# Two graph layers on one core: left weight sums queued behind evictions, and a last block worked by quarters

## The chip, the cores and the metric

The kernel runs on one core of one Trainium2 chip. The metric is the device time of one execution in microseconds; of several runs the median is taken. A core has TensorE (PE; PEld is its weight load), VectorE (DVE), ScalarE (ACT), GpSimd (POOL) and SyncE (SP). SP, ACT and POOL also issue DMAs.

## The reference, cut to what matters

128 graphs of 64 nodes with 768 features, all float32. Two layers, each with a residual and a layer norm. The first layer weighs neighbours by the similarity of the features; the second is an attention of 12 heads of 64 features, masked by the same adjacency.

```python
# layer 0: x is 128 x 64 x 768, adj 128 x 64 x 64 (zeros and ones)
p = softmax(x @ x.T / sqrt(768)); delta = p * adj
attn = delta / (sum(delta) + 1e-10)
ctx = upper(attn) @ (x @ Wl.T + bl) + diag(attn) * (x @ Ws.T + bs) + lower(attn) @ (x @ Wr.T + br)
x = layernorm(x + relu(layernorm(ctx, 1e-12) * gamma + beta), 1e-5)
# layer 1: q, k, v in 12 heads
s = q @ k.T / 8 + beta1 * adj, or -9e15 where adj is 0
x = layernorm(x + heads(softmax(s) @ v), 1e-5)
```

## The kernel before

The 8192 rows are cut into 16 blocks (`NBLK`) of 512 rows; a block is 4 tiles (`T`) of 128 rows, and a tile holds two graphs of 64 rows.

**Products by seven.** A block times a 768x768 weight is cut into 2x2 parts and formed by seven products instead of eight (`seven`, L365), in the order `ORDER` = 1, 2, 6, 5, 7, 4, 3, each for two halves of 128 rows (`j` = 0, 1). That makes 14 steps; a step is named below by product and half, as (7,1), and the steps are also counted as places 0 to 13. Products 1, 6, 7 and 4 gather in one PSUM bank per half (X), products 2, 5 and 3 in another (Y). After products 1, 6 and 7 VectorE reads X into an SBUF tile `u` (`first`, L413 to L416); the product that follows in that bank has to wait for this. After products 2, 7, 4 and 3 `last` writes a finished part. For this the kernel needs sums of the parts of each weight: `prepare` (L198) loads four quarters of a weight, and `formed` (L231) makes sums 5, 6, 7 and 4 on VectorE, in three instructions where a matrix lies in three pieces (L234) and in one where it is whole (L236). `store` sends them to DRAM for later blocks.

**Order of work.** Every step ends in `step()` (L137), which takes work from three queues: `first`, `urgent` and `lazy`. A plain item is VectorE work, and only one such item is taken per step; items marked `act`, `gap` or `tiny` can go beside it; an item marked `root` waits until `urgent` has no `act` item left; an item marked `free` is taken for nothing. `settle(key)` empties the queues up to a key, and `freed()` empties `first`. Hooks of a step are called ahead of its matmuls. The first blocks are traced for the Tile scheduler, which moves instructions of an engine by when it takes them to be ready; `tc.issue_after(ins)` fixes that what is traced in it goes behind `ins` on that engine, in issue order only. The last sums of the self weights are bound so already (`formed7`, L242). From L1022 on the order is the written one.

**The start.** The attention of block 0, the self part of block 0 (`self_part(0)`), during whose steps the sums of the self weights, the softmax of block 0 and then the sums of the left weights leave the queues (`prepare("l", wst, prep, (2, 1, 0))`, with two idle items ahead of sum 5 and one ahead of sum 6), then the left part (`side_part(0, "l")`) and the right part.

**The last block** (n = 15). `projected` forms q and k for three groups of heads (`hg`); `scores` (L817) multiplies them, VectorE scales, masks and shifts, ScalarE takes the exponentials in 16 pieces of 32x256 (L853), written transposed by 32x32 blocks, and VectorE transposes within the blocks (L857). `values` (L761) forms v by the seven products. The weighted sums multiply 64x64 weights of a graph with 64 rows of v and a column of ones; two graphs of a tile lie in the two halves of the partitions. Before the change v has to have head parity, not the graph, in its partition half. In earlier blocks three copies of ScalarE swap this; in the last block `values(..., in_place=True)` evicts in quarters of 64x192 instead (L779):

```python
for r in range(2):
    for g in range(2):
        rows = slice(g * L, (g + 1) * L)
        nc.vector.tensor_tensor(v[r * L : (r + 1) * L, t, g, heads, 0:HD],
                                pairs(ps)[rows, r], add[rows, r], ALU.add)
```

`weighted` (L866) does one group of heads for tiles 0 and 1 or for tiles 2 and 3; `added` then takes a reciprocal of the ones' sums (L888) and four instructions 128x64 that divide and add to the residual (L892), for each of two PSUM tiles. Two of six such calls are hooks of the values (places 12 and 13), four come after. `finish_by_act` normalises tiles on ScalarE (sums L937, squares L940, root L918, norm L926) with stores by POOL (L930): block 14 as `lazy` work in the last values, then tiles 2 and 3 of block 15. `finish` does tiles 0 and 1 on VectorE (statistics L353, aggregate L354, norm L950) with stores by SP (L951).

The functions that the change touches, and their callers:

Of the kernel before, what the change touches and what calls it, by code (L numbers as in the profile page):

```python
# [17 lines left out]
P = 128  # L18
# [5 lines left out]
T = 4  # L24
# [27 lines left out]
def gnn_two_layers(ctx: ExitStack, tc, x, adj, wl, bl, ws, bs, wr, br, gamma, beta,  # L52
# [145 lines left out]
    def prepare(nm, quarter_pool, sum_pool, waits=(0, 0, 0), queue=lazy):  # L198
# [30 lines left out]
                                        in_=in_sbuf[i][1][:, :, hg * P : (hg + 1) * P])  # L229

        def formed(i, out, left, right):  # L231
            if any(a[1] is None for a in (out, left, right)):
                for k in range(HC):
                    nc.vector.tensor_tensor(out[0][k], left[0][k], right[0][k], ALU.subtract)  # L234
            else:
                nc.vector.tensor_tensor(out[1], left[1], right[1], ALU.subtract)  # L236
            store(i)

        def idle():
            pass  # L240
# [517 lines left out]

        return one, two

    def values(n, hooks={}, in_place=False):  # L761

        def pairs(a):
            return a.rearrange("p (j r d) -> p r j d", r=2, d=HD)

        def last(t, h, ps, part):  # L770
            add = pairs(bias["v"][:, h * HALF : (h + 1) * HALF] if part is None else part)
            heads = slice(h * 3, (h + 1) * 3)
            if not in_place:
                nc.vector.tensor_tensor(v[:, t, :, heads, 0:HD], pairs(ps), add, ALU.add)
                return
            for r in range(2):
                for g in range(2):
                    rows = slice(g * L, (g + 1) * L)
                    nc.vector.tensor_tensor(v[r * L : (r + 1) * L, t, g, heads, 0:HD],  # L779
                                            pairs(ps)[rows, r], add[rows, r], ALU.add)  # L780

        by_tokens("v", blocks[n]["S"], last, None, hooks)
        if not in_place:
            low, high = v[0:L, :, 1, :, 0:HD], v[L:P, :, 0, :, 0:HD]
            swap = l0t.tile([P, T, HP, HD], F32, tag="lr", name="swap")
            later(("v", n), act(lambda: nc.scalar.copy(swap[0:L], high)), act(lambda: nc.scalar.copy(high, low)),
                  act(lambda: nc.scalar.copy(low, swap[0:L])), queue=urgent)
# [29 lines left out]
    def scores(n, hg, at_once=1, pool=None, gaps=1):  # L817

        blk = blocks[n]
        q, k = blk["qk"]
        settle("e")
# [21 lines left out]
        def exponentials(groups):  # L845
            if 0 in groups:
                blk["eT", hg] = (pool or l1e_p).tile([P, T, 2, P], F32, tag="lr" if pool else "eT", name="eT")
            e = blk["eT", hg].rearrange("p t c i -> p (t c) i")
            for a in groups:
                rows = slice(a * Q, (a + 1) * Q)  # L850
                for b in range(P // Q):
                    cols = slice(b * Q, (b + 1) * Q)
                    nc.scalar.activation(e[cols, :, rows], pairs[rows, :, cols], AF.Exp)  # L853

        def turn(h):
            e = blk["eT", hg][:, h * 2 : h * 2 + 2].rearrange("p t c i -> p (t c i)")
# [6 lines left out]
              *[act(partial(exponentials, range(a, a + at_once))) for a in range(0, P // Q, at_once)], *[GAP] * gaps,  # L863
              *([partial(turn, 0), partial(turn, 1)] if pool is None else [lambda: (turn(0), turn(1))]), queue=urgent)

    def weighted(n, hg, halves=range(2), heads=range(2)):  # L866


        blk = blocks[n]
        settle(("v", n))  # L870
        settle(("e", n, hg))
        freed()
        xt, eT = blk["x"], blk["eT", hg]
        y = {(r, h): ps_mm.tile([P, 2, 2, HD + 1], F32, tag="mm", name=f"ps_y{r}") for h in halves for r in range(2)}
        for h in halves:
            for t in range(2):
                for c in heads:
                    for r in range(2):
                        rows = slice(r * L, (r + 1) * L)
                        for g in range(2):  # L880
                            cols = slice(g * L, (g + 1) * L)
                            nc.tensor.matmul(y[r, h][cols, t, c, :], lhsT=eT[rows, 2 * h + t, c, cols],  # L882
                                             rhs=v[rows, 2 * h + t, g, hg + c * HC, :], start=True, stop=True)

        def added(h, r):
            ps = y[r, h][:, :, heads[0] : heads[-1] + 1, :]
            rz = st.tile([P, 2, 2], F32, tag="rz1", name="rz1")[:, :, 0 : len(heads)]
            nc.vector.reciprocal(rz, ps[:, :, :, HD])  # L888
            for t in range(2):
                res = xt[2 * h + t].rearrange("p (c k r d) -> p r c k d", c=2, k=HC, r=2)  # L890
                for k, c in enumerate(heads):
                    nc.vector.scalar_tensor_tensor(res[:, r, c, hg, :], ps[:, t, k, 0:HD], rz[:, t, k : k + 1],  # L892
                                                   res[:, r, c, hg, :], ALU.mult, ALU.add)

        later(("y", n, hg), *[partial(added, h, r) for h in halves for r in range(2)], queue=first)

    def finish_by_act(n, tiles=range(T), queue=urgent):

        xt, key = blocks[n]["x"], ("f", n)
        total, nm, var, std, rstd, shift = (st.tile([P, T], F32, tag=f"f{k}", name=f"f{k}") for k in range(6))  # L900
        some = slice(tiles[0], tiles[-1] + 1)

        def sums(fs):
            if queue is lazy:
                unused = l0t.tile([P, 2, D], F32, tag="lr", name="unused")[:, 0, :]
            else:
                unused = l1s_p.tile([P, T * 4 * L], F32, tag="s", name="unused")[:, 0:D]
            for t in tiles:
                fs(t, unused)

        def mean():
            nc.vector.tensor_scalar(nm[:, some], total[:, some], -1.0 / D, None, ALU.mult)

        def variance():
            nc.vector.tensor_scalar(std[:, some], var[:, some], 1.0 / D, 1e-5, ALU.mult, ALU.add)

        def root():
            nc.scalar.activation(std[:, some], std[:, some], AF.Sqrt)  # L918

        def factors():  # L920
            nc.vector.reciprocal(rstd[:, some], std[:, some])
            nc.vector.tensor_tensor(shift[:, some], nm[:, some], rstd[:, some], ALU.mult)

        def norm(ts):
            for t in ts:
                nc.scalar.activation(xt[t], xt[t], AF.Identity, bias=shift[:, t : t + 1], scale=rstd[:, t : t + 1])  # L926

        def stored(ts):
            for t in ts:
                nc.gpsimd.dma_start(out=out_t[n, t], in_=xt[t])  # L930

        def act(f):
            return f, "act" if queue is urgent else "root"

        settle(("y", n, 0))
        settle(("y", n, 1))
        later(key, (partial(sums, lambda t, o: nc.scalar.activation(o, xt[t], AF.Identity,  # L937
                                                                    accum_out=total[:, t : t + 1])), "after"),
              GAP, GAP, tiny(mean),
              act(partial(sums, lambda t, o: nc.scalar.activation(o, xt[t], AF.Square, bias=nm[:, t : t + 1],  # L940
                                                                  accum_out=var[:, t : t + 1]))),
              GAP, GAP, tiny(variance), act(root), GAP, tiny(factors),
              *[act(partial(norm, tiles[k : k + 2])) for k in range(0, len(tiles), 2)],
              (partial(stored, tiles[0:2]), "free"), GAP, GAP, (partial(stored, tiles[2:]), "free"), queue=queue)

    def finish(n, tiles=range(T)):
        xt = blocks[n]["x"]

        def norm(t, mean, rstd):
            nc.vector.tensor_scalar(xt[t], xt[t], mean, rstd, ALU.subtract, ALU.mult)  # L950
            nc.sync.dma_start(out=out_t[n, t], in_=xt[t])  # L951

        for t, mr in zip(tiles, moments(("f", n), [xt[t] for t in tiles], 1e-5, urgent)):
            later(("f", n), partial(norm, t, *mr), queue=urgent)

# [66 lines left out]
    for n in range(NBLK):  # L1024
# [20 lines left out]
        if p >= 0:  # L1045
# [2 lines left out]
            at(one, 5, weighted, p, 1)  # L1048
            if not last and m < DEEP:
                at(left, 13, weighted, p, 2)  # L1050
                at(right, 0, finish_by_act, p)
            elif not last:
                at(right, 1, weighted, p, 2)
                at(right, 2, finish_by_act, p)
            else:
                at(qk[1], 5, weighted, p, 2)

# [92 lines left out]
        for hg in range(NHG):  # L1150
            projected(n, hg, qk[hg])

    n = NBLK - 1
    values(n, {0: [partial(finish_by_act, n - 1, queue=lazy)], 4: [partial(scores, n, 2, 2, l0t)],
               12: [partial(weighted, n, 0, (1,))], 13: [partial(weighted, n, 1, (1,))]}, True)
    settle(("f", n - 1))
    settle(("y", n, 0))
    settle(("y", n, 1))
    weighted(n, 2, (1,))
    settle(("y", n, 2))  # L1160
    finish_by_act(n, range(2, 4))
    step()
    for hg in range(NHG):
        weighted(n, hg, (0,))
        settle(("y", n, hg))
        step()
        step()
    finish(n, range(2))
    settle(("f", n))


# [29 lines left out]
```

## Time and profile before

| what | us |
|---|---|
| median of 3 runs | 2934.7 |
| lowest and highest run | 2934.53, 2936.67 |
| profiled execution | 2938.14 |
| its span, first to last instruction | 2936.4 |
| TensorE busy | 2879.9 (98%) |
| VectorE busy | 1989.5 (68%) |
| ScalarE busy | 1123.6 (38%) |
| GpSimd busy | 729.9 (25%) |
| mean granted TensorE clock | 0.995 of full speed |

Times inside the kernel are counted from the start of the span. The busy time of an engine is a sum over stages with different limits; so the stages are read one by one below. A fp32 matmul shows as two passes ("x12" is six matmuls), and the ends of matmuls are modelled, so starts are compared with starts.

### The profile page before, as it was taken

Reading aid. Unit: us, or ns where it says so; the run is one execution under the profiler, and the core shown is the slowest. Engines: PE = TensorE matmul, PEld = TensorE weight load, DVE = VectorE, ACT = ScalarE, POOL = GpSimd, SP = SyncE. Lnnn points to the kernel's source line nnn. Section 1 sums busy time; section 2 is a strip of 40 time slices with the busy share of each in tenths; the row PEclk is TensorE's granted clock in tenths of the full one; section 3 lists DMA queues with packets and bytes.
Section 4 is the critical chain, followed back from the end, with each engine's and each line's share of the span. In section 5 each row is a group of like instructions: output and inputs, shape, how many; then the busy total and the mean of one; then the engine's idle time right before and its main releaser. Section 6 shows DMA issues by size and latency. Waiting matters only on the chain.

```text
span 2936.4 us, 49944 instructions
## 1 busy us (share of the span) xinstructions
PE 2879.9 (98%) x17578; PEld 1935.1 (66%) x17578; DVE 1989.5 (68%) x4034; ACT 1123.6 (38%) x2114; POOL 729.9 (25%) x879
## 2 busy tenths in 40 slices
PE   8999999999999999999999999999999999999997
PEld 5657567585665856658576575766757567585685
DVE  5678677676676766667667576666767667676656
ACT  0004324354243543434444344443434424354254
POOL 3133122304132130411405124051230413313110
PEclk9999999999999999999999999999999999999998
DMA  9788786849578595775958759486694966849442
GB/s 322 221 274 276 234 233 194 249 138 290 154 197 248 144 285 152 214 231 163 271 147 239 203 175 271 135 260 183 185 260 137 282 163 198 244 139 287 140 127 90
DMA packets 440278, 613.18 MB, mean 209 GB/s; under 512 B 53584, under 2 KB 416720, under 8 KB 440032
## 3 DMA queue, kind: packets, MB, share of 16 engines
q1 hardware_dynamic: 362096, 493.57, 56.0%
q10 hardware_dynamic: 60848, 44.05, 8.2%
q0 software_dynamic: 17088, 72.37, 6.7%
q8 instruction: 143, 2.34, 0.3%
q14 instruction: 103, 0.84, 0.1%
HBM read 539.43 MB, written 77.27 MB: 210 GB/s over the span
## 4 chain that ended last, share of the span: by engine, by line
PE 91%; ACT 3%; POOL 2%; DVE 2%; DMA 1%; issue 1%; SPq 0%; ACTq 0%; DVEq 0%
PE ps_X L384 35%; PE ps_Y L384 26%; PE ps_Y L638 11%; PE ps_X L638 10%; PE ps_ctx L677 3%; ACT eT L853 2%; PE sc L835 2%; PE ps_y L882 2%; PE u L527 2%; POOL q L337 1%; ACT L853 1%; ACT uqk L804 1%; POOL q L336 0%; PE ps_x L286 0%; DVE o L892 0%
## 5 line engine op out<-in xcount | busy, mean ns | idle before, releaser
L384 PE MATMUL ps_X<-xT,wqk 128*128 128x256 f32 x1728 | 395.9, 381 | 9.6 <-ACT uqk L804 9.6
L853 ACT ACTIVATE eT<-s 32x256 f32<-32x256 f32 x768 | 317.8, 414 | 184.7 <-DVE s L862 174.6
L384 PEld LDWEIGHTS ps_X<-xT,wqk 128*128 128x128 f32 x1728 | 325.8, 190 | 67.1 <-ACT uqk L804 16.2
L317 POOL TENSOR_TENSOR S<-hT 128x768 f32<-128x768 f32 x16 | 28.9, 1808 | 1133.4 <-PE ps_Y L384 1102.2
L384 PE MATMUL ps_Y<-S,wqk 128*128 128x256 f32 x1152 | 264.3, 379 | 0.0
L682 ACT ACTIVATE unused<-o 128x768 f32<-128x768 f32 x60 | 50.6, 843 | 500.4 <-DVE o L679 304.9
L384 PEld LDWEIGHTS ps_Y<-S,wqk 128*128 128x128 f32 x1152 | 218.9, 190 | 29.8
L438 DVE TENSOR_TENSOR lr<-ps_Y,u_deep 128x384 f32<-128x384 f32 x273 | 152.1, 557 | 108.6 <-PE ps_Y L638 82.8
L638 PE MATMUL ps_Y<-wlr,q 128*128 128x384 f32 x546 | 208.6, 491 | 0.0
L384 PE MATMUL ps_X<-wv,xT 128*128 128x384 f32 x576 | 195.0, 489 | 0.0
L804 ACT ACTIVATE uqk<-ps_X,bq 128x256 f32<-128x256 f32 x144 | 68.3, 474 | 324.9 <-PE ps_X L384 323.7
L812 DVE TENSOR_TENSOR q<-ps_Y,uqk 128x256 f32<-128x256 f32 x144 | 61.0, 424 | 177.7 <-ACT uqk L804 89.4
L384 PE MATMUL ps_X<-ws,hT 128*128 128x384 f32 x540 | 179.4, 486 | 0.1
L892 DVE SCALAR_TENSOR_TENSOR o<-ps_y,rz,o 128x64 f32<-128x64 f32 x768 | 165.0, 277 | 6.8
L638 PE MATMUL ps_X<-wlr,q 128*128 128x384 f32 x364 | 151.1, 497 | 14.5 <-POOL q L337 5.9
L384 PEld LDWEIGHTS ps_X<-wv,xT 128*128 128x128 f32 x576 | 108.2, 190 | 80.8 <-issue 8.4
L438 DVE TENSOR_TENSOR u_deep<-ps_X,lr 128x384 f32<-128x384 f32 x195 | 107.3, 550 | 68.0 <-PE ps_X L638 66.4
L384 PEld LDWEIGHTS ps_X<-ws,hT 128*128 128x128 f32 x540 | 102.4, 190 | 71.8 <-DMA ws<-in_L_gnn_W_self_dram 0.7
L638 PEld LDWEIGHTS ps_Y<-wlr,q 128*128 128x128 f32 x546 | 101.6, 190 | 67.2
L415 DVE TENSOR_TENSOR u<-ps_X,bv 128x384 f32<-128x384 f32 x96 | 53.4, 556 | 130.3 <-PE ps_X L384 130.2
L384 PE MATMUL ps_X<-S,wqk 128*128 128x256 f32 x576 | 138.2, 385 | 0.0
L384 PE MATMUL ps_Y<-xT,wqk 128*128 128x256 f32 x576 | 135.6, 385 | 0.0
(247 smaller groups left out, 5482.6 us busy)
## 6 DMA issues: line engine op xcount, KB each, us to landing
wlr<-lr_d SPq DMA_DIRECT2D x819, 192.0 KB, 3.5
wqk<-qk_d SPq DMA_DIRECT2D x672, 192.0 KB, 2.4
wv<-d_v SPq DMA_DIRECT2D x192, 192.0 KB, 3.3
ws<-d_s SPq DMA_DIRECT2D x180, 192.0 KB, 6.0
wv<-in_L_gnn_Wv_dram SPq DMA_DIRECT2D x144, 192.0 KB, 4.1
ws<-in_L_gnn_W_self_dram SPq DMA_DIRECT2D x135, 192.0 KB, 5.5
xa<-in_x_dram SPq DMA_DIRECT2D x64, 384.0 KB, 5.4
out_dram<-o POOLq DMA_DIRECT2D x62, 384.0 KB, 6.2
```

Of the source, the lines that this page charges most:

```text
L384: nc.tensor.matmul(ps, lhsT=a, rhs=b, start=(c == 0 and i in (1, 2, 5)), stop=(c == len(fs) - 1), skip_group_check=True)
L415: recent["u"] = evicted[nm] = nc.vector.tensor_tensor(u, ps, bias[nm][:, b * HALF : (b + 1) * HALF], ALU.add)
L438: nc.vector.tensor_tensor(dst, view(ps), add, ALU.add)
L527: nc.tensor.matmul(u[g * L : (g + 1) * L, t, :], lhsT=xT[:, c, tok], rhs=xT[:, c, tok], start=(c == 0), stop=(c == KC - 1))
L638: nc.tensor.matmul(ps, lhsT=a, rhs=b, start=(k == 0 and j in (1, 2, 5)), stop=(k == len(fs) - 1), skip_group_check=True)
L677: nc.tensor.matmul(ps[g * L : (g + 1) * L, 0:HALF], lhsT=blk["aT"][:, t, g * L : (g + 1) * L], rhs=blk["lr"][t][:, g, cols], start=True, s ...
L804: nc.scalar.activation(u, ps, AF.Identity, bias=bias["qk"[j]][:, c : c + 1])
L812: nc.vector.tensor_tensor(dst, ps, part, ALU.add)
L835: nc.tensor.matmul(sc[r][g * L : (g + 1) * L, t, c, :], lhsT=q[rows, c, tok], rhs=k[rows, c, tok], start=True, stop=True)
L853: nc.scalar.activation(e[cols, :, rows], pairs[rows, :, cols], AF.Exp)
L882: nc.tensor.matmul(y[r, h][cols, t, c, :], lhsT=eT[rows, 2 * h + t, c, cols], rhs=v[rows, 2 * h + t, g, hg + c * HC, :], start=True, stop= ...
L892: nc.vector.scalar_tensor_tensor(res[:, r, c, hg, :], ps[:, t, k, 0:HD], rz[:, t, k : k + 1], res[:, r, c, hg, :], ALU.mult, ALU.add)
```

## The change

Three things are changed. The sums of the left weights are bound, with `tc.issue_after`, behind the eviction that was traced last when they leave the queue. In the last block v stays with its graph in the partition half (evictions of 128x384), and the exponentials are written so that the weights match it; the weighted sums go by quarters (two tiles, half of the features), of which three are called from hooks of the values (places 10, 11, 13) and one after; each quarter divides with two 128x384 instructions of VectorE into a tile `shares`, and adds of 128x384 by POOL or VectorE bring it to the residual; the scores of the last group are called at place 2 instead of 4. The statistics of all four tiles are taken by VectorE, nearly all behind the last eviction, and normalised by ScalarE (three tiles) and VectorE (one). The stores of the last block and of block 14 are all issued by SP, and block 14's squares no longer wait for the exponentials. `finish_by_act` becomes `finish`; for the other blocks its order and its engines stay.

```diff
         def formed(i, out, left, right):
+            with tc.issue_after(recent["u"].ins) if nm == "l" else ExitStack():
+                subtracted(out, left, right)
+            store(i)
...
-    def values(n, hooks={}, in_place=False):
+    def values(n, hooks={}, stay=False):
...
-            if not in_place:
-                nc.vector.tensor_tensor(v[:, t, :, heads, 0:HD], pairs(ps), add, ALU.add)
-                return
-            for r in range(2):
...
+            nc.vector.tensor_tensor(v[:, t, :, heads, 0:HD], pairs(ps), add, ALU.add)
...
-                    nc.scalar.activation(e[cols, :, rows], pairs[rows, :, cols], AF.Exp)
+                    to = (b, a) if n < NBLK - 1 else (a // 2 * 2 + b % 2, b // 2 * 2 + a % 2)
+                    to = [slice(k * Q, (k + 1) * Q) for k in to]
+                    nc.scalar.activation(e[to[0], :, to[1]], pairs[rows, :, cols], AF.Exp)
...
-                nc.gpsimd.dma_start(out=out_t[n, t], in_=xt[t])
+                (nc.sync if ends else nc.gpsimd).dma_start(out=out_t[n, t], in_=xt[t])
...
+        if ends:
+            begin = (summed, "after"), GAP, (lambda: (mean(), squared()), "act"), GAP, GAP, tiny(variance), act(root), GAP, GAP, GAP, tiny(factors)
...
+    def quarter(h, c):
...
+        y = [ps_mm.tile([P, 2, NHG, HD + 1], F32, tag="mm", name=f"ps_y{r}") for r in range(2)]
+        for r in range(2):
+            for k in range(NHG):
+                for t in range(2):
+                    for g in range(2):
+                        rows = slice(g * L, (g + 1) * L)
+                        nc.tensor.matmul(y[r][rows, t, k, :], lhsT=blk_e[k][rows, 2 * h + t, c, r * L : (r + 1) * L],
+                                         rhs=v[rows, 2 * h + t, r, c * HC + k, :], start=True, stop=True)
...
+        def divided(r):
+            rz = small[:, 2 * h : 2 * h + 2, 32 + 8 * c + 4 * r : 32 + 8 * c + 4 * r + NHG]
+            nc.vector.reciprocal(rz, y[r][:, :, :, HD])
+            nc.vector.tensor_tensor(by_head[:, :, r], y[r][:, :, :, 0:HD],
+                                    rz[:, :, :, None].to_broadcast([P, 2, NHG, HD]), ALU.mult)
+
+        def added(t, engine):
+            res = xt[2 * h + t][:, c * HALF : (c + 1) * HALF]
+            engine.tensor_tensor(res, res, share[:, t, :], ALU.add)
...
+    def behind(h, c):
...
+        later(("q", h, c), partial(divided, 0), lambda: (divided(1), added(0, nc.gpsimd), added(1, nc.gpsimd)),
+              queue=first)
...
+    def before_last():
+        divided, added = quarter(1, 0)
+        measured(0, 0)
+        divided(0)
+        divided(1)
+        added(0, nc.gpsimd)
+        added(1, nc.vector)
...
-    values(n, {0: [partial(finish_by_act, n - 1, queue=lazy)], 4: [partial(scores, n, 2, 2, l0t)],
-               12: [partial(weighted, n, 0, (1,))], 13: [partial(weighted, n, 1, (1,))]}, True)
+    values(n, {0: [partial(finish, n - 1, queue=lazy)], 2: [partial(scores, n, 2, 2, l0t)],
+               10: [partial(behind, 0, 0)], 11: [partial(behind, 1, 1)],
+               12: [freed], 13: [before_last]}, True)
     settle(("f", n - 1))
-    settle(("y", n, 0))
-    settle(("y", n, 1))
-    weighted(n, 2, (1,))
-    settle(("y", n, 2))
-    finish_by_act(n, range(2, 4))
-    step()
-    for hg in range(NHG):
-        weighted(n, hg, (0,))
...
+    divided, added = quarter(0, 1)
+    for t, c in ((3, 1), (2, 1), (1, 0)):
+        measured(t, c)
+    for t in (3, 2):
+        measured(t, 0)
+        whole(t)
+    factors(slice(2, 4))
+    divided(0)
+    inverse(slice(2, 4))
+    for t in (3, 2):
+        norm_by_act(t)
+    divided(1)
+    added(1, nc.gpsimd)
+    added(0, nc.vector)
+    for t in (0, 1):
+        measured(t, 1)
+        whole(t)
+    factors(slice(0, 2))
+    inverse(slice(0, 2))
+    nc.vector.tensor_scalar(xt[0], xt[0], mv[:, 0, 0:1], rstd[:, 0], ALU.subtract, ALU.mult)
+    nc.sync.dma_start(out=out_t[n, 0], in_=xt[0])
+    norm_by_act(1)
```

`measured(t, c)` is one statistics instruction over half a tile, `whole` its aggregate, `factors` adds epsilon and takes the root on ScalarE, `inverse` takes the reciprocal and the shift, and `norm_by_act` normalises on ScalarE and issues the store by SP.

## The prediction

> **What bounds the kernel now.** I read the page first, then the timeline and the granted clock of the first 60 us, then the chain that ended last and the timeline from 2880 us on, since the diff touches only these two ends.
>
> ```profile
> PE 2879.9 (98%) x17578; PEld 1935.1 (66%) x17578; DVE 1989.5 (68%) x4034; ACT 1123.6 (38%) x2114; POOL 729.9 (25%) x879
> ```
>
> TensorE is busy in 98% of the span, so between the ends only its work counts. The 56 us in which it is not busy, and the stretches in which its clock is low, are what a change of order can win. The timeline of the start (start, duration, engine, line, operands; in brackets the idle time before and its releaser):
>
> ```profile
> 29.72 1.49 DVE L234 TENSOR_TENSOR t_l<-b_l 128x384 f32<-128x384 f32 x3
> 31.78 4.14 PE L384 MATMUL ps_X<-b_s,hT 128*128 128x384 f32 x12
> ...
> 34.46 1.03 DVE L234 TENSOR_TENSOR t_l<-b_l,t_l 128x384 f32<-128x384 f32 x2 [0.80 <-DMA b_l<-in_L_gnn_W_left_dram]
> 35.40 1.49 DVE L234 TENSOR_TENSOR b_l<-b_l 128x384 f32<-128x384 f32 x3
> ...
> 36.81 1.49 DVE L234 TENSOR_TENSOR t_l<-b_l,t_l 128x384 f32<-128x384 f32 x3
> 38.22 0.55 DVE L415 TENSOR_TENSOR u<-ps_X,bs 128x384 f32<-128x384 f32 x1
> ...
> 38.82 7.16 PE L384 MATMUL ps_X<-t_s,hT 128*128 128x384 f32 x12 [2.90 <-DVE u L415]
> ...
> 49.68 4.03 PE L384 MATMUL ps_X<-b_l,hT 128*128 128x384 f32 x12
> ```
>
> The matmuls of product 7 of the self part are through at 35.9, but its eviction (L415) stands behind the sums of the left weights (L234) on VectorE, some of them waiting for a load, until 38.22. TensorE waits 2.9 us and then takes 7.16 us for 12 passes that take 3.87 us from start to start elsewhere. The granted clock of four stretches (busy us per engine, then clock, DMA share) shows why:
>
> ```profile
> 36.00:39.00 3.00, 0.18 (x1) 0.18 (x2) 2.97 (x7) 0.00 (x0) 2.33 (x5) 0.85 1.00 367
> 39.00:46.00 7.00, 7.00 (x13) 3.87 (x14) 1.93 (x4) 0.00 (x0) 0.96 (x3) 0.58 1.04 402
> ```
>
> The end, by the chain that ended last (start, duration, what):
>
> ```profile
> 2898.66 1.95 PE ps_X L384 x6
> 2900.63 0.57 DVE u L415
> ...
> 2909.71 2.15 PE ps_Y L384 x6
> ...
> 2924.18 0.86 DVE o L892 x4
> ...
> 2931.05 0.68 DVE o L950
> ```
>
> From 2900.6 on the end is nearly all VectorE: quartered evictions of the values (L779, 4 x 0.36), then normalised sums of the last block (L892), then statistics. TensorE ends its values at 2914.6; the other 21.8 us of the span have no product of a weight left.
>
> **The change, part by part. Sums of the left weights.** The 12 instructions of L234 (0.5 us each) stay; each group of three now follows the eviction traced last before it. By the queue's rules (one VectorE item per step; the self sums, then the softmax, then two idle items) the groups come at the steps of (7,1), (4,1), (3,0), (3,1): product, half. So the second eviction of product 6 runs at 29.8 instead of 33.1, the first of product 7 at 33.9 instead of 38.2, and product 4, due at 16.19 + 10 x 1.935 = 35.5, finds its bank read. All 14 steps then run without a gap: 16.19 + 14 x 1.935 = 43.3 where the left part starts, against 49.7: 6.4 us, of which 3.3 are the slow passes (7.16 - 3.87) and 3.1 idle. The moved 6 us of VectorE lie beside products 4, 3 and the left part's first (VectorE worked 4.3 us of 39 to 54). Of what waits for them: the left part needs the sum of its product 6 at 43.3 + 7.7 = 51.0, and it is formed by about 42; the stores of these sums by POOL move back by some 8 us, with the copy `lr_d<-d_l` and the stores `d_r<-t_r` (now 53.6) queued behind them; nothing on TensorE reads those before 100 us. Right weights are needed at 70.7 and their loads end their issue at 50.3 even now. Cost 0; without this cover, up to 1.5 us per group. Ends: 3.1 (idle alone) to 6.5. I take 6.4, as nothing else in the first 60 us idles TensorE after 16.2.
>
> [...]
>
> **The values of the last block.** Unquartered evictions cost 0.56 instead of 1.46 (L774 against L779): 8 x 0.9 = 7.2 us off VectorE, which was the bound from 2900.6 on. TensorE then paces: 14 x 1.935 = 27.1 from 2881.7, scores 1.15, and three quarters of the weighted sums among the products where two sixths were. A quarter is 48 passes of 64x64. Weighted sums take 17 ns a pass now (64 in 1.09) over four corners of the array; the quarter uses only the two where row and column group agree, nearest to `u`, which uses two column groups: 96 in 2.95, 31 ns. So 1.5 + 0.25 for entry, three times 5.2. Ends: 17 ns (2.1 less in all) and 46 ns, the cold rate in the tail now (32 in 1.46; 2.2 more).
>
> Scores move from place 4 to 2 and the squares of block 14 (4 x 1.06 on ScalarE) go ahead of its 16 exponentials: those run 2895.4 to 2902.1, the transposes (2 x 0.7) to 2903.4. TensorE reaches the first quarter at 2902.2, does two head groups, waits 0.7 for the third. Sum: 2881.7 + 27.1 + 1.15 + 5.2 + 0.7 = 2915.9 for the last values matmul, 1.3 later than now.
>
> **After the last eviction.** VectorE is free of it at 2916.7. Then three statistics (0.49 each, L353), two more with aggregates (0.71 each), epsilon 0.2: 2919.8, root on ScalarE beside the next division (reciprocal 0.2 + 128x384 from PSUM 0.6), inverse 0.36: 2920.9; second division 2921.7. POOL's add of one tile (1.0, as L452) ends at 2922.9; VectorE's own add 0.56, statistics and aggregate of tile 0 run beside it. Then tile 1: 0.7, epsilon, root, inverse 0.85, norm on ScalarE 1.0 (L926): 2925.6. TensorE's fourth quarter, done by 2918.6, is covered.
>
> An add with two SBUF inputs may clash with POOL's. The row is L757, at its shortest 0.43 us alone and 1.91 in the median, beside POOL's sums. I add 0.6 (ends 0 and 1.0): 2926.2. [...]
>
> From the last norm (2932.3 now) to the end of the span takes 4.1 us, two stores by SP with two of POOL's just before; kept, as four stores again fall within 4 us. So 2930.3 against 2936.4: 6.1 us, from 3.5 (cold-rate quarters, full clash) to 8.0 (17 ns, none). Stores moved to SP cost 0: SP's last load is issued by 2885.5, block 14's stores wait for norms that end by 2913, and those of block 15 come after. On POOL they would have stood (4 x 0.54 from 2922.0) in front of the adds; that is the cover lost if they stayed.
>
> Other blocks keep their instructions. **Sum: 6.4 + 6.1 = 12.5**; span 2936.4 to 2923.9, the profiled execution (2938.1, 1.7 us around the span) to 2925.6; the median of the runs, 3.4 below that execution, from 2934.7 to 2922.2.
>
> **Rivals.** (1) The start gives nothing: another VectorE item takes the place of the sums, or a binding set at trace time leaves the sums early. Against: the eviction is traced before the group, and nothing else is ready there. Only the end counts: 2928.6.
> (2) The end gives nothing: TensorE loses its clock at the third head group's wait and does the rest (4 steps 7.7, quarters 4.5) at half rate, 12 us more, which eats 6.1 and more if it does not recover. Against: it idled 1.4 and 1.3 us around 2907 with the clock at 1.00. It needs a wait of some 2.9 us where I see 0.7; a wait of 2 with half of this: 2928.3, start alone.
> (3) Slower: the loads become the bound. From 120 to 200 us the DMA share is 0.8 to 1.0; a TensorE that comes 6.4 us earlier could wait for weights, lose these 6.4, and drop its clock at each wait of 2.9 us (3.3 us each). Four or more such stretches make 13 us: 2934.7 + 13 - 6.1 = 2941.6. It decides from the point where loads land after the step that needs them. Against: TensorE waits for a DMA only in the first 10 us, and the load queue itself mostly waits for TensorE's buffers (L409 for ps_X, 83.6 us in 70 waits up to 450), so loads come earlier too.
> (4) Nothing moves in sum: 2934.7.
>
> **How the numbers follow.** Forecast 0.70, its own range 2920 to 2926.5 (gains 8.2 to 14.5); rival 1 0.10, rival 2 0.10, rival 3 0.06, rival 4 0.04. Runs of the kernel before differ by 2.1 us, so no change can be told within about 0.2%, 5.9 us. Rivals 1 and 2 lie at this bound, counted 0.12 faster and 0.08 same. Faster 0.82, same 0.12, slower 0.06. For 8 in 10 the range ends at the rivals of one part alone, 2928.8, and 1.5 us below the forecast's low end, 2918.5.
>
> **What would show it.** The start: no L234 between evictions of products 6 and 7, 12 passes of product 4 in 3.87 us, clock 1.00 from 36 to 46, left part at 43.3. The end: L774 in all values, a wait under 1 us in the first quarter, last values matmul near 2909.5 (2915.9 - 6.4), last norm some 10 us later. Wrong would be: TensorE idle in a new place before 200 us, a quarter over 2 us, VectorE idle between last eviction and norms for more than 1 us in all.

## The result and the profile after

The changed kernel takes 2924.3 us (median of 5 runs, 2923.7 to 2927.0) against 2934.8 us for the kernel before on the same chip (5 runs, 2934.5 to 2937.1). The ratio is 0.996, its 95% interval 0.995 to 0.997: faster by 10.5 us, where 12.5 were predicted. The profiled execution of the changed kernel is an average one (2923.8 us, span 2922.1), that of before was 3.3 us above its median; so the two spans differ by 14.3 us, and stages are compared by their lengths below.

The page's line of the engines, busy us and share of the span:

```profile
PE 2872.4 (98%) x17578; PEld 1931.7 (66%) x17578; DVE 1979.6 (68%) x3973; ACT 1120.4 (38%) x2107; POOL 732.2 (25%) x879
```

TensorE has the same 17578 instructions and 7.5 us less busy time: passes that ran at a granted clock of 0.50 are gone, among them 6.83 us of the start and 3.41 us near 330 us, the latter by chance (the middle of the span, below). Its timeline at the start (start us, duration, engine, line, operation, operands):

```profile
30.66 4.03 PE L389 MATMUL ps_X<-b_s,hT 128*128 128x384 f32 x12
34.53 4.03 PE L389 MATMUL ps_X<-t_s,hT 128*128 128x384 f32 x12
38.40 4.03 PE L389 MATMUL ps_Y<-b_s,S 128*128 128x384 f32 x12
42.27 4.03 PE L389 MATMUL ps_X<-b_l,hT 128*128 128x384 f32 x12
```

Product 4 (the second line) starts 3.87 us after the one before it and takes no longer than the others; the wait of 2.90 us and the 7.16 us are gone. VectorE's timeline shows where the sums of the left weights went (in brackets the idle time before and its releaser):

```profile
32.80 0.56 DVE L420 TENSOR_TENSOR u<-ps_X,bs 128x384 f32<-128x384 f32 x1 [3.11 <-PE ps_X L389]
...
34.73 0.56 DVE L420 TENSOR_TENSOR u<-ps_X,bs 128x384 f32<-128x384 f32 x1 [0.78 <-PE ps_X L389]
...
35.80 1.49 DVE L240 TENSOR_TENSOR t_l<-b_l 128x384 f32<-128x384 f32 x3
37.20 0.55 DVE L596 TENSOR_TENSOR o<-ps_X,bs 128x384 f32<-128x384 f32 x1
...
39.08 1.49 DVE L240 TENSOR_TENSOR t_l<-b_l,t_l 128x384 f32<-128x384 f32 x3
```

The two evictions of product 7 (L420) now run at 32.80 and 34.73, each as soon as TensorE has its half; the first is the one for which product 4 waited until 38.22 before. Each group of three sums (L240) stands behind an eviction. The windows show the clock (window, its length, busy us of PE, PEld, DVE, ACT and POOL, then clock, DMA share, GB/s); in the second window it was 0.58 before:

```profile
36.00:39.00 3.00, 3.00 (x10) 1.72 (x10) 2.15 (x5) 0.00 (x0) 0.53 (x1) 1.00 1.01 285
39.00:46.00 7.00, 7.00 (x23) 4.17 (x22) 5.96 (x13) 0.00 (x0) 2.68 (x5) 1.00 1.05 393
```

The end, by the chain that ended last (start, duration, what):

```profile
2903.85 0.57 DVE shares L1179
2904.42 0.07 issue
2904.49 1.36 POOL o L1184
2905.86 5.05 issue
2910.90 1.42 POOLq L1278
2912.32 0.02 issue
2912.34 0.57 DVE small L1197
...
2914.07 1.03 ACT o L1211
```

The chain ends with the norm on ScalarE at 2915.10. The span ends at 2922.1, 7.0 us later, and the two stores of the last tiles do not fill that: they are issued at 2914.60 and 2915.12 and land by 2917.9. The windows of the last 4 us hold neither an engine's work nor a DMA:

```profile
2918.00:2920.00 2.00, 0.00 (x0) 0.00 (x0) 0.00 (x0) 0.00 (x0) 0.00 (x0) 0.50 0.00 0
2920.00:2922.10 2.10, 0.00 (x0) 0.00 (x0) 0.00 (x0) 0.00 (x0) 0.00 (x0) 0.50 0.00 0
```

What lies there is in the instructions of the kernel's closing line, L1278 (queue, operation, count; shortest, median and longest ns; first and last start):

```profile
L1278 POOLq DRAIN  x3: 40/93/10407, 2910.9 to 2921.8; - x3
L1278 SPq DRAIN  x3: 7/7/7, 2918.0 to 2921.6; - x3
```

The line has two drains each on the queues of PEld, DVE and ACT as well. SP's first comes at 2918.0, when the last store has landed. POOL's first one starts with its last sum at 2910.9 and takes 10.41 us, until 2921.3; only then do the others close, at 2921.6 (SP waits another 3.4 us in one piece). In the kernel before, the same line was

```profile
L1197 POOLq DRAIN  x3: 40/93/3480, 2930.3 to 2936.2; - x3
L1197 SPq DRAIN  x3: 7/7/7, 2935.6 to 2935.9; - x3
```

where POOL's drain took 3.48 us and was over at 2933.8, before SP's last store had landed. So the two stages at the ends gave this between the two profiles: from the first self product to the left part 33.5 us before, 27.4 after (6.05 less); from the start of the last block's values to the end of the span 54.7 before, 50.2 after (4.5 less). The other 3.8 us between the spans are 1.4 before the first product and 2.4 in the 2830 us between; that middle is between 2829.6 and 2832.1 us in the profiles of this study. About 1.7 of the 2.4 us (an estimate, half the length of the piece) are a piece of low clock that comes and goes with the execution, not with the change: in the profile of before the granted clock was 0.50 from 328.3 to 331.7 us, in that of the changed kernel it was 1.00 there. Five of the twelve profiles (before, e1, e2, e5, e9) have such a piece, 3.41 us long and between 321 and 332 us, and their middles are 2831.1 to 2832.1 us; those of the other seven are 2829.6 to 2830.5. The changed kernel has it in e5 and not in its first profile.

### The profile page after: what moved, and what is told of

It is laid out like the page before. It is cut to its first block, busy times and chain, and to the rows that moved or that the text cites. A ratio compares the mean times of both kernels' runs of the same rounds, so it can differ in the third digit from the quotient of the medians.

```text
span 2922.1 us, 49871 instructions
## 1 busy us (share of the span) xinstructions
PE 2872.4 (98%) x17578; PEld 1931.7 (66%) x17578; DVE 1979.6 (68%) x3973; ACT 1120.4 (38%) x2107; POOL 732.2 (25%) x879
## 4 chain that ended last, share of the span: by engine, by line
PE 93%; ACT 3%; POOL 2%; DVE 1%; issue 1%; DMA 0%; POOLq 0%; SPq 0%; ACTq 0%
PE ps_X L389 36%; PE ps_Y L389 27%; PE ps_Y L643 11%; PE ps_X L643 10%; PE ps_ctx L682 3%; ACT eT L853 2%; PE sc L833 2%; PE ps_y L882 2%; PE u L532 2%; POOL q L342 1%; ACT L853 1%; ACT uqk L801 1%; PE ps_x L291 0%; POOL q L341 0%; POOL q L343 0%
## 5 line engine op out<-in xcount | busy, mean ns | idle before, releaser
L892 DVE SCALAR_TENSOR_TENSOR o<-ps_y,rz,o 128x64 f32<-128x64 f32 x720 | 154.7, 278 | 6.4
L420 DVE TENSOR_TENSOR u<-ps_X,bv 128x384 f32<-128x384 f32 x96 | 53.4, 557 | 132.5 <-PE ps_X L389 132.5
```

The lines of the kernel that those rows point to most:

```text
L420: recent["u"] = evicted[nm] = nc.vector.tensor_tensor(u, ps, bias[nm][:, b * HALF : (b + 1) * HALF], ALU.add)
```

## The experiments

Three things were to be settled: whether each part alone gives its share, what ends the new kernel, and why POOL's drain is long. For the last, the theories were that a sum of POOL as its last work makes the drain long, that the drain is long when POOL has issued no store for a long time, and that it is of no account, SP's stores being what ends the kernel. Ratios are to the kernel before on the same chip, with the 95% interval.

| kernel | median us | ratio (95%) | POOL's drain, us |
|---|---|---|---|
| before | 2934.8 to 2935.6 | 1 | 3.48 |
| changed | 2924.3 | 0.996 (0.995 to 0.997) | 10.41 |
| e1, start alone | 2930.1 | 0.9983 (0.9974 to 0.9991) | 3.50 |
| e2, end alone | 2930.0 | 0.9981 (0.9972 to 0.9990) | 10.41 |
| e3, last sums by VectorE | 2921.4 | 0.9954 (0.9941 to 0.9966) | 10.40 |
| e4, before with a POOL sum last | 2935.9 | 1.0003 (0.9994 to 1.0011) | 3.45 |
| e5, changed, again | 2924.5 | 0.9965 (0.9952 to 0.9977) | 10.41 |
| e6, one last store by POOL | 2924.2 | 0.9962 (0.9948 to 0.9975) | 3.01 |
| e7, block 14's stores by POOL | 2922.0 | 0.9957 (0.9944 to 0.9969) | 2.93 |
| e8, e3 with a statistic earlier | 2921.2 | 0.9952 (0.9939 to 0.9964) | 10.40 |
| e9, spare POOL store early | 2923.2 | 0.9955 (0.9938 to 0.9971) | 2.16 |
| e10, spare POOL store last | 2921.1 | 0.9950 (0.9935 to 0.9965) | 2.23 |

**e1: the start alone** (the kernel before with this edit only)

```diff
         def formed(i, out, left, right):
+            with tc.issue_after(recent["u"].ins) if nm == "l" else ExitStack():
+                subtracted(out, left, right)
+            store(i)
...
-            store(i)
```

> The kernel before with the binding of the left sums alone. If the start's gain is its own (the profiled starts are 16.19 to 49.68 before and 14.83 to 42.27 after the change, 6.0 us shorter), the median falls by about 6.0 us, the granted clock from 36 to 46 us is 1.00, and the end keeps its length. Rival: the shift of the later work against loads or clock windows adds or takes something; then the gain is not 6.0, and the middle of the span is longer or shorter than before by the difference.

Measured: 2930.1 us, 5.5 less than before. TensorE's timeline has product 4 and the left part where the changed kernel has them, 3.87 us a product:

```profile
36.58 4.03 PE L389 MATMUL ps_X<-t_s,hT 128*128 128x384 f32 x12
40.45 4.03 PE L389 MATMUL ps_Y<-b_s,S 128*128 128x384 f32 x12
44.31 4.03 PE L389 MATMUL ps_X<-b_l,hT 128*128 128x384 f32 x12
```

The stage from the first self product to the left part is 27.2 us. In its end, which is the old one, a group of the values after the wait for quartered evictions took 3.89 us:

```profile
2901.85 1.61 PE L887 MATMUL ps_y<-v,eT 64*64 64x65 f32 x16 [1.27 <-DVE v L784]
2903.39 3.89 PE L389 MATMUL ps_Y<-wv,S 128*128 128x384 f32 x6
```

In the profile of before the same six passes took 2.20 us after a wait of 1.28. So the old end varies, by 1.7 us, with the clock (0.84 in the window 2900 to 2911 here, 1.00 in the same stretch of before). What the text above calls clock windows are, in the traces, pieces of low clock like this one, at 0.50 for 3.41 us, or for two times that (6.83 us at the start of before).

**e2: the end alone** (the changed kernel without the binding)

```diff
         def formed(i, out, left, right):
-            with tc.issue_after(recent["u"].ins) if nm == "l" else ExitStack():
-                subtracted(out, left, right)
-            store(i)
...
+            store(i)
```

> The changed kernel without the binding of the left sums. If the two parts add up, the median falls by 10.5 less 6.0, 4.4 us, which is what the profiled stretch from the start of the last values to the end of the span lost (54.7 to 50.2 us); the slow passes around 40 us are back. Rival: the parts need each other; then it falls by clearly more or less than 4.4 us.

Measured: 2930.0 us, 5.6 less than before. The two parts alone give 5.5 + 5.6 = 11.1, both together 10.5 and 10.9 (in e5): they add up, and neither is empty. The 4.4 us expected of this part came from the one profile of before, whose end was a short one (below). The old start shows another form of the same stall, a wait of 3.70 us and 12 passes in 5.83:

```profile
39.69 5.83 PE L384 MATMUL ps_X<-t_s,hT 128*128 128x384 f32 x12 [3.70 <-DVE u L415]
```

The granted clock was 0.50 from 40.86 to 44.27 us here, for 3.41 us; in the profile of before it was so from 38.12 to 44.95, for 6.83 us.

**e3: the last sums by VectorE** (the changed kernel, at its fourth quarter)

```diff
     divided(1)
-    added(1, nc.gpsimd)
     added(0, nc.vector)
+    added(1, nc.vector)
```

> The changed kernel with both adds of the fourth quarter by VectorE, so that POOL's last work is its add at 2904.5 instead of the one at 2910.9. In the changed kernel POOL's closing drain lasts 10.41 us, to 2921.3, while SP has seen the last store land by 2918.0. Theory, the drain runs some 9 us beyond POOL's last sum and sets the end: the drain now ends near 2915, SP's stores set the end at about 2918.5 + 0.5 for the second add on VectorE, so 2.5 to 3.3 us less than the changed kernel. Rival, the drain ends late for another reason (the other engines' end, or a fixed closing time): no gain, and up to 0.5 us more than the changed kernel.

Measured: 2921.4 us, 14.2 less than before. The last norm ends 43.3 us after the values' start, as in the changed kernel (43.2), though VectorE does one sum more: POOL's sum was no shorter (1.37 us in the changed kernel) than VectorE's two in a row (1.02 us here). The end of the span is 47.1 after the values' start instead of 50.2. The closing line:

```profile
L1278 POOLq DRAIN  x3: 40/93/10403, 2905.2 to 2919.5; - x3
L1278 SPq DRAIN  x3: 7/7/7, 2918.9 to 2919.2; - x3
```

POOL's drain is as long as before this edit, but it starts with the sums of the third quarter at 2905.2 and is over at 2915.7; now SP, whose last store lands at 2918.85, ends the kernel.

**e4: the kernel before with a small POOL sum as its last work**

```diff
+    nc.gpsimd.tensor_tensor(side, side, side, ALU.mult)
```

> The kernel before with one more POOL instruction behind its last store: a product of a 128x128 constant tile with itself, whose result nobody needs (about 0.5 us). Theory, a closing drain behind a POOL sum takes some 9 us: POOL ends near 2931.5 + 9 = 2940.5 instead of 2933.8, and the span grows by about 5 us. Rival, the drain depends on something else (its length before, 3.48 us, follows the landing of POOL's own stores): no change beyond 0.3 us.

Measured: 2935.9 us, no different from before (1.0003, 0.9994 to 1.0011); the drain takes 3.45 us. So that a sum comes last does not make the drain long: that theory fell. The profile showed something else, the old stall without its slow passes:

```profile
31.64 4.03 PE L384 MATMUL ps_X<-b_s,hT 128*128 128x384 f32 x12
38.57 4.14 PE L384 MATMUL ps_X<-t_s,hT 128*128 128x384 f32 x12 [2.89 <-DVE u L415]
42.54 4.03 PE L384 MATMUL ps_Y<-b_s,S 128*128 128x384 f32 x12
```

The wait is 2.89 us, as in the profile of before (2.90), but the next 12 passes take 3.97 us from start to start and not 7.16, with the clock at 1.00.

**e5: the changed kernel again**, on the chip of e6 to e8 (no edit).

> The changed kernel once more, as the measure for the three that follow on the same chip. All theories: some 10 to 11 us below the kernel before; the closing drain of POOL lasts 10.4 us and ends about 3.4 us after the last store has landed. If the clock windows fall differently in each execution, the stretch from the first self product to the left part is again 27.2 to 27.5 us, since nothing waits in it.

Measured: 2924.5 us, drain 10.41 us: the same as at first.

**e6: one of the last two stores by POOL** (the changed kernel)

```diff
-    nc.sync.dma_start(out=out_t[n, 0], in_=xt[0])
+    nc.gpsimd.dma_start(out=out_t[n, 0], in_=xt[0])
```

> The changed kernel with the store of tile 0 by POOL, behind its last sum; the other seven stores stay with SP. Four profiles with a POOL store last had a drain of 3.45 to 3.50 us that ended 0.6 us after the landing of that store; four with a POOL sum last and no store near had 10.4 us from the issue of that sum. Theory A, the 10.4 us belong to a drain with no store of POOL's own shortly before: the drain ends 0.6 us after this store's landing, near 2918, and the end comes 3 us sooner than in the changed kernel. Theory B, the drain takes 10.4 us from POOL's last instruction once sums have run: it ends near 2925 and the kernel is 3 us slower than the changed one.

(The counts in this text are too high: until then three profiles had a POOL store near the end and three had none.) Measured: 2924.2 us, no gain. The drain took 3.01 us, as a store near it would have it, but what was won there was lost ahead of it. POOL's timeline:

```profile
2912.66 1.38 POOL L1184 TENSOR_TENSOR o<-o,shares 128x384 f32<-128x384 f32 x1 [5.08 <-DVE shares L1179]
2919.34 0.56 POOL L1249 DMA_DIRECT2D out_dram<-o  x1 [5.30 <-issue]
```

Tile 0 was normalised at 2916.3 (L1248, 2915.63 + 0.67). POOL issued its store at 2919.34, 3.0 us later and 5.30 us after its sum; in the last 3.0 us the profile shows nothing that it waited for. The store landed at 2922.0 and ended the kernel.

**e7: block 14's stores by POOL again** (the changed kernel)

```diff
-                (nc.sync if ends else nc.gpsimd).dma_start(out=out_t[n, t], in_=xt[t])
+                nc.gpsimd.dma_start(out=out_t[n, t], in_=xt[t])
```

> The changed kernel with the four stores of block 14 by POOL again, so that POOL's last store is issued some 5 to 8 us before its last sum at 2910.9. Theory A in its wide form (any store of POOL's in the last few tens of us is enough): the drain ends within 1 us of the last sum, near 2913, SP's stores set the end, 3 us sooner than the changed kernel. Theory A in its narrow form (the store must be under way when the drain begins, as in the kernel before with a sum behind its stores), and theory B: the drain is 10.4 us again, and the time that of the changed kernel.

Measured: 2922.0 us, 2.6 less than e5 on the same chip. The four stores left POOL at 2908.0 to 2909.7, later than expected since they queue behind its sums, and landed by 2913.9. The drain began at 2911.5 and took 2.93 us, until 2914.4, and SP ended the kernel. The stores were still under way when the drain began, so this run cannot tell the wide form of theory A from the narrow one; e9 does. The last sum of POOL is still there, at its old place.

**e8: e3, and one statistic ahead of the last eviction**

```diff
         added(1, nc.vector)
+        measured(3, 1)
...
-    for t, c in ((3, 1), (2, 1), (1, 0)):
+    for t, c in ((2, 1), (1, 0)):
         measured(t, c)
...
     divided(1)
-    added(1, nc.gpsimd)
     added(0, nc.vector)
+    added(1, nc.vector)
```

> Both adds of the fourth quarter by VectorE, as in the run with the last add by VectorE, and one more statistics instruction (tile 3, second half, 0.5 us) moved from behind the last eviction to the gap of 0.7 us ahead of it. If the end is VectorE's chain behind the last eviction and then SP's stores, it falls by 0.5 us against that earlier run and by 3.3 to 3.8 us against the changed kernel. Rival: the instruction delays the last eviction by what it does not find free there, and nothing is won against the earlier run.

Measured: 2921.2 us, 14.2 less than before on that chip and 3.3 less than e5. The statistic now lies in VectorE's wait for the last values (start, duration; then the eviction):

```profile
2906.35 0.55 DVE L1197 BATCH_NORM_STATS2 small<-o 128x6 f32<-128x384 f32 x1
2907.11 0.56 DVE L777 TENSOR_TENSOR v<-ps_Y,u 128x384 f32<-128x384 f32 x1 [0.21 <-PE ps_Y L389]
```

The last norm ends 42.9 us after the values' start, 0.45 earlier than in e3, one statistic's time. The runs cannot tell 0.2 us between e3 and e8. This version beats both kernels of the study.

**e9 and e10: a spare store of POOL, of 64 KB to a DRAM tile that nothing reads** (the changed kernel with this one store added: in e9 at place 4 of the last values, in e10 directly behind POOL's last sum)

```diff
+    spare = tc.dram_tile([P, P], F32, name="spare")
+
+    def spared():
+        nc.gpsimd.dma_start(out=spare, in_=ident)
...
-               10: [partial(behind, 0, 0)], 11: [partial(behind, 1, 1)],
+               4: [spared], 10: [partial(behind, 0, 0)], 11: [partial(behind, 1, 1)],
...
     added(1, nc.gpsimd)
+    spared()
     added(0, nc.vector)
```

(The middle edit is that of e9, the last that of e10.)

> The changed kernel with one spare store of 64 KB by POOL (the identity tile to a buffer that nobody reads) at place 4 of the last values, some 30 us ahead of POOL's last sum and landed long before its first. So far a closing drain with a store of POOL's own under way ended 0.5 to 0.6 us after its landing, and one with none under way and none for 220 us took 10.4 us. If a store under way is what makes the drain short, it is 10.4 us here and the time that of the changed kernel. If a store in the last tens of us is enough, the drain ends within 2 us of the last sum, and the kernel is 3 us faster than the changed one.

> The changed kernel with the same spare store directly behind POOL's last sum, with nothing of its own to wait for. With the store of tile 0 by POOL that store started 5.3 us after the end of the last sum, while its data was ready some 3 us sooner. If POOL needs those 5.3 us whenever it goes from sums to a store after a long time without one, the store starts near 2917.6, lands near 2920, the drain ends 0.6 us later, and the time is within 1 us of the changed kernel. If the 5.3 us were a wait for the data, the store starts within 2 us of the sum's end, the drain ends near 2917, and the kernel is 3 us faster.

Measured: e9 2923.2 us, e10 2921.1 us. In e9's timeline of POOL the store leaves 91 us ahead of the last sum, and five more sums stand between:

```profile
2822.68 0.56 POOL L1217 DMA_DIRECT2D spare<-ident  x1
...
2913.57 1.37 POOL L1184 TENSOR_TENSOR o<-o,shares 128x384 f32<-128x384 f32 x1 [5.08 <-DVE shares L1179]
```

The closing line of e9, then that of e10:

```profile
L1283 POOLq DRAIN  x3: 40/102/2157, 2913.5 to 2921.2; - x3
L1284 POOLq DRAIN  x3: 40/93/2229, 2914.4 to 2919.3; - x3
```

In e9 the drain takes 2.16 us from the last sum's start, 0.8 from its end (9.0 in the changed kernel), and from the values' start to the end of the span it is 46.9 us instead of 50.2. The runs show less than that, 12.4 us under before; the middle of the profiled execution, 2831.2 us, was 1.6 longer than that of the changed kernel: it has the piece of low clock, 0.50 from 321.9 to 325.3 us, that the changed kernel's first profile has not. In e10 the store leaves 1.33 us after the sum, the drain takes 2.23 us, and the values to the end take 46.9 us too. That is the second case of its expectation, but not for the reason given there, a wait for the data, since in e6 the data was ready 3.0 us before the store started:

```profile
2911.69 1.37 POOL L1184 TENSOR_TENSOR o<-o,shares 128x384 f32<-128x384 f32 x1 [5.08 <-DVE shares L1179]
2914.40 0.56 POOL L1217 DMA_DIRECT2D spare<-ident  x1 [1.33 <-issue]
```

**What follows for the drain.** In the five profiles in which POOL's last store lies 219 to 226 us ahead of the drain (changed, e2, e3, e5, e8) the drain takes 10.40 to 10.41 us; in the seven in which it lies within 91 us (before, e1, e4, e6, e7, e9, e10), 2.2 to 3.5. What comes last, sum or store, does not decide (e4, e9). That a recent store of POOL shortens the drain is shown by e9 (2.16 us) and e10 (2.23), which add nothing else; how old the store may be, between 91 and 219 us, no run shows. What POOL does in the 10.4 us is not shown either: the profile shows no other instruction of POOL in them. It stays open why the drain is 8.2 us shorter in e9 than in the changed kernel, which differ in the early store alone, and why e6's store left 5.30 us after the sum ahead of it where e10's left after 1.33 and e7's after 1.61, each the first for some 220 us.

## Why the prediction was right, and its one wrong term

**The start: the mechanism as predicted, the size in the upper half.** Predicted was a left part 14 x 1.935 = 27.1 us after the first self product; it is 27.2 to 27.4 in all nine profiles with the binding. The groups stand behind the evictions that were named, and the right weights' loads and the stores cost nothing: from the left part to the next stage it is 66.40 us both before and after. The 6.4 us came from one execution, though. Of the three profiles without the binding, the stage takes 33.5 (before), 32.9 (e2) and 30.4 (e4): the wait is 2.9 to 3.7 us in all three, but the slow passes behind it cost 3.3 us in the first, 1.8 in the second and 0.1 in the third. The granted clock says why: it was 0.50 for 6.83 us in the first, for 3.41 us in the second and not at all in the third, so that each piece of 3.41 us cost 1.6 to 1.8 us. The row of 7.16 us that the prediction counted from had two such pieces. So the mean is lower than the row, and the medians say 5.5 (e1 against before) and 4.9 to 5.3 (what the changed kernel and e5 save beyond e2). The prediction named both ends (3.1 for idle alone, 6.5) and took the row whole. A wait of 2.9 us was followed by slow passes in one execution (before) and not in another (e4); what decides it, no run shows.

**The end: all terms up to the last norm held, the closing did not.** From the start of the values (2871.87 in the profile after, 2881.7 before):

| term | predicted | measured |
|---|---|---|
| last values matmul ends | 34.2 | 33.8 |
| one quarter of 48 passes | 1.5 (31 ns a pass) | 1.54 (32 ns) |
| three quarters with their entries | 5.2 | 5.0 |
| wait for the third head group | 0.7 | none |
| last eviction ends | 35.0 | 34.4 |
| second division ends | 40.0 | 39.0 |
| clash of the two sums | 0.6 | 0.4 |
| last norm ends | 44.5 | 43.2 |
| last norm to the end of the span | 4.1 | 7.0 |
| sum | 48.6 | 50.2 |

(A quarter with its entry is what it adds between two products: from 2888.64 to 2894.15 it is 5.51 us for twelve passes and the first quarter, less 3.87 for the twelve; then 1.75 and 1.64.) The quarters' rate, for which only distant rows were there, came out near that of the row with two column groups. The first quarter, in the timeline of TensorE (the first line is its weight loads, in brackets their idle time before):

```profile
2888.64 4.03 PE L389 MATMUL ps_X<-wv,xT 128*128 128x384 f32 x12
...
2892.60 1.48 PEld L1169 LDWEIGHTS ps_y<-v,eT 64*64 64x64 f32 x48 [0.55 <-issue]
2892.61 1.61 PE L1169 MATMUL ps_y<-v,eT 64*64 64x65 f32 x48
2894.15 2.20 PE L389 MATMUL ps_X<-wv,xT 128*128 128x384 f32 x6
```

The 0.6 us for the clash of the two sums, with 1.0 as its upper end, was the author's estimate, and no run shows either. The runs showed 0.4: VectorE issued its sum first (2910.89) and took 0.56 us (two in a row with none of POOL's beside them took 1.02 in e3), and POOL's (2910.94) took 1.36 to 1.37 instead of the 0.99 of a sum with none of VectorE's beside it (e6, at 2904.83).

The step that failed is "From the last norm (2932.3 now) to the end of the span takes 4.1 us, [...] kept", with its companion "Stores moved to SP cost 0". The first names two stores by SP with two of POOL's just before, and with stores of POOL its closing was short, 2.93 us in e7, 2.16 in e9 and 2.23 in e10. The change left POOL with a sum 11 us before the end and no store in the 226 us before that, and its drain of 10.4 us became what ends the kernel: 2910.9 + 10.4 = 2921.3, against 2918.0 when SP was done. The term is 2.9 too small; 1.3 too much in the terms ahead of it hid part of this. With the drain short or early the term is 3.7 to 4.0 us (e3, e7 to e10), and the whole change 14.2 us in e3 and 14.5 in e10. Nothing in the profile of before showed the 10.4 us; but its closing line showed that POOL's drain was there and took 3.48 us, only 1.4 us from setting the end, and the prediction did not bound it when it moved POOL's work.

Against the runs the end's 6.1 us came out as 5.6 (e2 against before) and 5.0 to 5.4 (what the changed kernel and e5 save beyond e1), though the profiles give 4.5: the old end in the profile of before (54.7 us) was a short one, since its waits were not followed by slow passes; in e1 and e4, with 3.41 us at a clock of 0.50 from 2903.5 and 2904.4 on, it took 56.4 and 56.3. That the runs lie nearer to 6.1 than 4.5 does is luck of this kind, not a sign that the closing was right. Start and end erred for the same reason, in opposite senses: before's one profile had the start's slow passes and not the end's. The two ends of the forecast's range were not made alike: 14.5 adds the best of both parts, 8.2 is more than the sum of their worst, 3.1 and 3.5; the 10.5 measured lies inside either way.

**The rivals.** One part alone was put at 2928.6 and 2928.3; e1 and e2 show what that looks like, 2930.1 and 2930.0, so (1) and (2) did not happen. (2) had the quarters lose the clock: none of the first three comes over 0.2 us late, and the six passes after each take 2.20 us. The argument against it was weaker than it looked: the waits of 1.4 and 1.3 us around 2907 are one gap, seen once by the weight load (1.41) and once by the matmuls (1.28), and the clock stayed at 1.00 behind it in that execution only. Behind the same gap of 1.27 and 1.28 us six passes took 3.89 us in e1 and 3.53 in e4, so slow passes came there without a wait of some 2.9 us just ahead. The new end has no such gap: its longest wait of TensorE is 0.39 us. (3) had TensorE wait for weights: from 15 us on TensorE waits for no DMA, as before, and the stage behind the left part is the same to 0.01 us. (4) is excluded by the interval.

## What to carry to other kernels

Before work is moved off an engine, look at its closing drain as well as at its last instruction: the end here was the latest of several closings (POOL's drain at 2921.3 in the changed kernel, SP's last store at 2918.85 in e3), and one that is covered by 1.4 us in the old trace is a term of the sum. The stall at the start had no fixed price (3.3, 1.8 and 0.1 us of slow passes in three executions); take the slow passes of one profile as the upper end, the idle time alone as the lower one, and look at the same stall in other executions where there are any. The two elementwise sums at the very end were as well done by VectorE alone: POOL's share of them saved 0.1 us (43.2 against 43.3) and put POOL's closing of 10.4 us behind them.

## What the runs showed of the chip that was not expected

- POOL's closing drain took 10.40 to 10.41 us in the five profiles in which POOL's last store lay 219 to 226 us back, and 2.2 to 3.5 us in the seven in which it lay within 91 us; a spare store of 64 KB was enough (2.16 us in e9, 2.23 in e10). A store that POOL issues after a sum started 5.30 us after it in e6, where it first had 2.3 us to wait for its data, 1.33 us in e10 and 1.61 in e7; why is open.
- The same wait of 2.89 to 2.90 us left the clock at 1.00 in one execution and cost 3.3 us of slow passes in another (e4, before); six passes after a wait of 1.27 us took 3.89 us in e1, and 2.20 after 1.28 in before. The low clock came in pieces of 3.41 us at 0.50, one or two at a time, wherever it came while TensorE worked through the products (before, e1, e2, e4, e5, e9).
- Passes of 64x64 on two corners of the array took 32 ns each (48 in 1.54 us from start to start, the quarters of the changed kernel), those on four 17 ns (64 in 1.09 us, the weighted sums of earlier blocks in the profile of before).
